# One drain per slot as the signal for TensorE's products, in a two-layer image network with gathered sampling

## The chip, the cores and the metric

The kernel runs on one core of a Trainium2 chip, as one program. The metric is the device time of one execution in microseconds; with one core, that core's time is the kernel's time. Lower is better.

## The reference

The input is four images `x` of 128 channels and 128 x 128 pixels, in float32, and the output has the same shape. Two layers follow each other; each has a convolution and a feed-forward part (FFN), both with a normalisation in front and a residual add behind. Cut to what matters:

```python
# layer 0
x = x + deform_conv(_ln_c(x), w_off, w_conv)      # 3x3 taps, sampled at learned places
t = t + moe(_ln_t(t), router_w, router_b, expert_w, expert_b)   # top 2 of 8 experts, per token
# layer 1
x = x + fft_conv(_ln_c(x), alphas, betas)         # mixes channels in the frequency domain
t = t + soft_moe(_ln_t(t), gate_w, gate_b, weight1, weight2)    # 64 experts take their top 8 tokens each

# deform_conv: offsets by a 3x3 convolution, then for each tap k
py, px = base_y + dy[k], base_x + dx[k]
sampled[k] = sum(weight(corner) * x[:, corner] for the four pixels around (py, px))
out = einsum('bckhw,ock->bohw', sampled, w_conv)
```

In layer 0 every pixel reads nine places of the image, each blended from four neighbouring pixels. The places depend on the data, so these reads are gathers. In layer 1's FFN each of 64 experts takes, over an image's 16,384 tokens, the eight with the highest gate.

## The kernel before

**Tiling.** The unit of work is a *slot*. A slot samples one row of 128 pixels at three of the nine taps. Each image has 32 groups of four rows, and each group has 12 slots (four rows by three sets of taps), so four images make 4 x 32 x 12 = 1536 slots. A class `Chunk` holds what a slot does:

- `gather` (L737): three indirect DMAs issued by GpSimd (POOL), one per tap, each fetching 128 places x 4 corners x 128 channels from a table in DRAM into the tile `g`. The pool of `g` has `AHEAD` = 7 buffers (L82, L245), so up to seven slots' gathers are in flight.
- `weighted` (L750) on VectorE (DVE) and `weighted_too` (L758) on ScalarE (ACT): each corner times its blending weight, in place in `g`. The tile `spread` holds the weights.
- `summed` (L766): twelve 128 x 128 transposes on TensorE, which add up the four corners of each tap in PSUM, in the tile `trg`. They are the last readers of `g`: after them the buffer is free for the gather of seven slots later.
- `moved` (L780): ACT copies `trg` to `sT` in SBUF. Every fourth `moved` starts `convolved`, in which TensorE multiplies `sT` by the weights of the convolution (`sums`).

What follows the sampling of a group (normalisations, routing, the eight experts `pe`, layer 1's mixing and gates `pq`), and the preparation of the next image's offsets and table, are Python generators called *jobs*. They are resumed slot by slot and put their matmuls, copies and vector work between those of the sampling, so that the whole kernel is one interleaved stream. Behind the last slot come the 64 experts of layer 1 for the last image, and a pass that turns the tokens back into channels and writes the output.

**What sets the order.** Nothing is reordered: `InOrder` (L91 to L103) wraps each engine and records every instruction with `keep_in_program_order` (L101, hence the "L101" in every row of the profile). Each engine's queue holds its instructions in the order in which Python issues them. The order inside a slot n is written out in the main loop (L1588 to L1636): `weighted` of slot n+1, `moved` of slot n-2, the jobs' due steps (`turns.steps`, L1603), `weighted_too` of n+1, `summed` of n, the jobs' matmuls (`turns.fills`, L1611), and last the gathers of slot n+7, by `next(source)` (L1635).

**PSUM and the two-slot hop.** A job's or a slot's products go to one of `BANKS` = 6 PSUM buffers (L83, L246); `fills` (L147) keeps the count of those in use. A job that has issued matmuls waits `turns.hop` slots before it issues what reads them. The hop is 2 in the slots (L1584) and 1 behind them (L1638). So by the written order, readers of a product come two slots after it.

**Synchronisation.** An instruction that another engine (or, for hazards, its own) depends on raises its engine's semaphore when it is done, and the dependent one waits for a value of it. The tile framework derives all these waits and updates from the tiles read and written. Before, 6022 of TensorE's 31,271 matmuls carry such an update.

Of the kernel before, what the change touches and what calls it, by code (L numbers as in the profile page):

```python
# [90 lines left out]
class InOrder:  # L91


    def __init__(self, tc, engine):
        self.tc, self.engine = tc, engine

    def __getattr__(self, name):
        issue = getattr(self.engine, name)

        def issued(*args, **kwargs):  # L100
            return self.tc.keep_in_program_order(issue(*args, **kwargs))  # L101

        return issued  # L103


class Engines:
    def __init__(self, tc):
        nc = tc.nc
        self.tensor, self.vector = InOrder(tc, nc.tensor), InOrder(tc, nc.vector)
        self.scalar, self.gpsimd = InOrder(tc, nc.scalar), InOrder(tc, nc.gpsimd)  # L110
        self.sync = InOrder(tc, nc.sync)

# [57 lines left out]
def runs_of(runs, first, step):  # L170


    if len({n for _, _, n in runs}) > 1:
        return [(slice(s, s + n), first(y, n)) for s, y, n in runs]
    (_, y, n), (_, z, _) = runs
    ap = first(y, n)
    dims = list(ap.ap)
    return [
        (
            slice(0, 2 * n),  # L180
            bass.AP(ap.tensor, ap.offset, [dims[0], [(z - y) * step, 2]] + dims[1:]),
        )
    ]
# [3 lines left out]
def metaformer_kernel(  # L187
# [16 lines left out]
    nc = tc.nc  # L204
# [33 lines left out]
    with ExitStack() as main:  # L238
# [15 lines left out]
        eng = Engines(tc)  # L254
# [5 lines left out]
        class Image:  # L260


            def __init__(self, b):
                self.b = b
                self.table = tabs.tile([TW * TC, 2 * P], F32, name=f"table{b}", tag="table")
                self.grid = self.table.rearrange("(i j) e -> i j e", j=TC)
                self.index = pw.tile([P, P, TAPS], I32, name=f"index{b}", tag="index")
                self.weight = {}
                self.xc = {}
                self.z = {}  # L270
                self.tails = {}


                self.read = self.normed = self.continued = self.sent = 0
                self.offsets = self.placed = self.known = 0
                self.left = 0
                self.direct = P // RB
                self.rooms = {}
# [381 lines left out]
        def table_of(im, pitch):  # L660

            base = turns.slot
            im.left = P // RB + 1 + P // CB
            for t in range(P // RB + 1):
                while turns.slot < base + int(t * pitch):
                    yield 1
                turns.start(block(im, t))

        def later_offsets(im):
            for t in range(im.direct, P // RB):  # L670
                turns.start(again(im, t))
                yield SPACE


        class Group:
# [6 lines left out]
            def begin(self):  # L682
                self.xg = pb.tile([P, 4, P], F32, name="xg", tag="xg")
                for s, rows in runs_of(
                    self.runs,
                    lambda y, n: x[self.b, :, y : y + n, :].rearrange("c y x -> c (y x)"),
                    P,
                ):
                    eng.sync.dma_start(
                        out=self.xg[:, s, :].rearrange("p s x -> p (s x)"), in_=rows  # L690
                    )
# [854 lines left out]
        def biases():  # L1546

            for whole, bias, to, n in (
                (HID, weight1[:, P, :], b1T, NJ),
                (P, weight2[:, HID, :], b2T.unsqueeze(1), 1),  # L1550
            ):
                rows = late.tile([E1, whole], F32, name="rows", tag="two", bufs=3)
                eng.sync.dma_start(out=rows, in_=bias)
                yield 3
                yield FILL
                pbt = bank([P, n, E1], "pbt")
                for j in range(n):
                    eng.tensor.transpose(
                        pbt[:, j, :],
                        rows.rearrange("e (p j) -> e j p", j=n)[:, j, :],  # L1560
                        ident[:E1, :E1],
                    )
                yield turns.hop
                eng.vector.tensor_copy(to, pbt)
# [22 lines left out]
        n = -1  # L1587
        while n < total + 3 or turns.jobs:  # L1588
            turns.slot = start + n
            b, k = divmod(n, slots)  # L1590
            if n == 0:
                turns.start(later_offsets(first))
            lag = 0 if b else SPACE * (P // RB - AFTER + 2)
            if k == lag and b + 1 < NB:
                images[b + 1] = Image(b + 1)
                images[b + 1].border()
                pitch = (slots - AHEAD - BLOCK - lag) / (P // RB)
                turns.start(table_of(images[b + 1], pitch))
            if n + 1 < total:
                chunk[n + 1].weighted()  # L1600
            if 0 <= n - 2 < total:
                chunk[n - 2].moved()
            turns.steps()  # L1603
            if n >= 0 and n + 3 < total and (n + 3) % 12 == 0:
                chunk[n + 3].row.group.weights((n + 3) // 12 % 2)
            if n + 1 < total and chunk[n + 1].shared:
                chunk[n + 1].weighted_too()
            if 0 <= n < total:
                chunk[n].summed()
                turns.fill()  # L1610
            turns.fills(0)  # L1611
            if n == LATE * slots:

                phase_a.close()
                late = main.enter_context(tc.tile_pool(name="late", bufs=2, side="right"))
                b1T = late.tile([P, NJ, E1], F32, name="b1T", tag="b1T", bufs=1)
                b2T = late.tile([P, E1], F32, name="b2T", tag="b2T", bufs=1)
                turns.start(biases(), later=True)
                part = lambda: late.tile([P, 2, HID], F32, name="w", tag="w", bufs=4)

                rooms = [[part(), part()], [part(), part()], flat_pads]
                rooms.append([pw.tile([P, 2, HID], F32, name="w", tag="index")])
                for _ in range(2):
                    rooms[-1].append(
                        pw.tile([P, 1, HID], F32, name="w", tag="weight", bufs=3 * P // CB // 2)
                    )
                middle = Experts(range(LATE), Weights(lambda i: rooms[i % 4]), 4, 2)
                middle.part = part
                middle.streams = 2
                middle.weights.load(4)  # L1630
                middle.start()
            if 0 <= n - 2 < total:
                chunk[n - 2] = None
            if 0 <= n and len(chunk) < total:
                chunk.append(next(source))  # L1635
            n += 1  # L1636
            if n == total + 2:
                turns.hop = 1  # L1638

                sampling.close()  # L1640
                own = main.enter_context(tc.tile_pool(name="own", bufs=OWN))

                flat = lambda w: w[:, 0:8, :].rearrange("p (n q) c -> p n (q c)", q=4)
                others = [
                    flat_pads,
                    [(late, f"{tile}{b}") for tile in ("tok", "share") for b in (1, 2)],
                    [flat(wconv_sb), flat(ew_sb)],
                ]

                def room(i):  # L1650
                    i %= OWN + 3 + len(LEFT)
                    if i < OWN:
                        return own.tile([P, EC, HID], F32, name="w", tag="w")
                    i -= OWN
                    if i == 1:
                        return [
                            pool.tile([P, 1, HID], F32, name="w", tag=tag, bufs=1)
                            for pool, tag in others[1]
                        ]
                    if i < 3:  # L1660
                        return others[i]
                    return [
                        pb.tile([P, n, HID], F32, name="w", tag=tag, bufs=bufs)
                        for tag, n, bufs in LEFT[i - 3]
                    ]

                ending = Ending(range(LATE, NB), Weights(room), OWN + 2, 1)
                ending.part = lambda: own.tile([P, 2, HID], F32, name="w", tag="w")
                ending.streams = OWN // 2
                ending.among = False  # L1670
                turns.start(ahead())
                ending.start()
# [39 lines left out]
```

## Time and profile before

| | before |
|---|---|
| median of three runs | 7361.9 us (7357.83 to 7363.09) |
| the profiled execution | 7358.05 us |
| its span, first to last instruction | 7356.1 us |
| TensorE's granted clock, mean | 0.896 |
| TensorE matmuls | 6006.3 us busy (82%), 31,271 instructions |
| VectorE | 4789.5 us (65%), 16,100 |
| GpSimd | 4432.3 us (60%), 4691 |
| ScalarE | 3707.7 us (50%), 9999 |
| bytes moved by DMA | 1524.69 MB, mean 207 GB/s |

All times are of one execution, taken by the hardware profiler. PE is TensorE's matmuls and PEld its weight loads. In a row of a group, "out<-in xcount | busy, mean ns | idle before, releaser" gives the tiles, the number of instructions, their busy time, the mean length of one, and how long the engine stood idle just before them, with what ended most of that. "issue" as releaser means that the profile shows nothing that the engine waited for; "remote" is a releaser without a name. Matmuls are pipelined: their ends are modelled, and their records overlap, so PE's busy share isn't its share of peak. Releasers are inferred from semaphore events.

### The profile page before, as it was taken

Reading aid. Unit: us, or ns where it says so; the run is one execution under the profiler, and the core shown is the slowest. Engines: PE = TensorE matmul, PEld = TensorE weight load, DVE = VectorE, ACT = ScalarE, POOL = GpSimd, SP = SyncE. Lnnn points to the kernel's source line nnn. Section 1 sums busy time; section 2 is a strip of 40 time slices with the busy share of each in tenths; the row PEclk is TensorE's granted clock in tenths of the full one; section 3 lists DMA queues with packets and bytes.
Section 4 is the critical chain, followed back from the end, with each engine's and each line's share of the span. In section 5 each row is a group of like instructions: output and inputs, shape, how many; then the busy total and the mean of one; then the engine's idle time right before and its main releaser. Section 6 shows DMA issues by size and latency. Waiting matters only on the chain. (4 is left out here: it accounts for less than half of the span.)

```text
span 7356.1 us, 103037 instructions
## 1 busy us (share of the span) xinstructions
PE 6006.3 (82%) x31271; PEld 3981.9 (54%) x31271; DVE 4789.5 (65%) x16100; ACT 3707.7 (50%) x9999; POOL 4432.3 (60%) x4691
## 2 busy tenths in 40 slices
PE   5788888887888888887888888888877788788885
PEld 3455555555555555555555555555555555555553
DVE  5466666676667666666667666667667665566663
ACT  4345555554555555554455555555444444444452
POOL 1666666666666666666666666666666665666641
PEclk7888999998898998998899999898898999899897
DMA  6666666666666666666666666666666677677777
GB/s 204 191 200 212 204 207 210 202 194 188 197 201 203 205 206 200 204 193 186 193 209 200 207 202 201 198 199 210 186 189 181 201 250 238 180 247 237 246 236 273
DMA packets 578917, 1524.69 MB, mean 207 GB/s; under 512 B 86424, under 2 KB 225408, under 8 KB 578368
## 3 DMA queue, kind: packets, MB, share of 16 engines
q0 software_dynamic: 369664, 1210.35, 55.0%
q1 hardware_dynamic: 206400, 299.36, 12.1%
q10 hardware_dynamic: 2304, 8.39, 0.3%
q8 instruction: 254, 4.16, 0.2%
q14 instruction: 295, 2.42, 0.1%
HBM read 1380.92 MB, written 136.85 MB: 206 GB/s over the span
## 5 line engine op out<-in xcount | busy, mean ns | idle before, releaser
L101 POOL DMA_INDIRECT g<-table,index x4608 | 4377.4, 950 | 2710.4 <-issue 1190.9
L101 PEld LDWEIGHTS trg<-ident,g 128*128 128x128 f32 x18432 | 2300.2, 150 | 1501.3 <-issue 1288.2
L101 PE MATMUL trg<-ident,g 128*128 128x128 f32 x18432 | 2575.2, 288 | 562.9 <-issue 465.9
L101 DVE SCALAR_TENSOR_TENSOR x<-pe,scaled,x 128x128 f32<-128x128 f32 x4048 | 1379.7, 341 | 1432.5 <-remote 644.6
L101 DVE TENSOR_TENSOR g<-g,spread 128x1024 f32<-128x1024 f32 (+1 forms) x1536 | 2129.1, 1387 | 202.4 <-DMA g<-table,index 90.0
L101 ACT COPY sT<-trg 128x384 f32<-128x384 f32 x1536 | 720.5, 472 | 2742.1 <-remote 1187.4
L101 PE MATMUL sums<-sT,wconv_sb 128*128 128x512 f32 x2304 | 1326.6, 658 | 53.1 <-issue 50.9
L101 ACT ACTIVATE g<-g,weight 128x128 f32<-128x128 f32 x4096 | 1306.3, 394 | 1.9 <-DMA g<-table,index 1.7
L101 PE MATMUL pe<-ew_sb,x1T 128*128 128x512 f32 x2048 | 1163.6, 649 | 147.0 <-issue 88.6
L101 PEld LDWEIGHTS sums<-sT,wconv_sb 128*128 128x128 f32 x2304 | 435.1, 208 | 518.9 <-issue 516.5
L101 PEld LDWEIGHTS pe<-ew_sb,x1T 128*128 128x128 f32 x2048 | 343.7, 205 | 261.1 <-issue 182.3
L101 ACT ACT_TABLE_LOAD x270 | 346.4, 1283 | 23.5 <-DVE nmax L101 9.8
L101 PE MATMUL sums<-xg,ident 128*128 128x512 f32 x256 | 163.8, 726 | 125.8 <-ACT x1T L101 96.8
L101 DVE TENSOR_TENSOR x<-ps,x 128x512 f32<-128x512 f32 x128 | 88.1, 688 | 264.5 <-remote 119.6
L101 PE MATMUL po<-pad,woff_sb 128*64 128x512 f32 x768 | 216.1, 645 | 17.8 <-issue 11.0
L101 DVE TENSOR_TENSOR x<-x,pe 128x512 f32<-128x512 f32 x128 | 87.0, 679 | 217.8 <-remote 130.4
L101 PE MATMUL pl<-rw_sb,x1T 128*128 128x8 f32 x1024 | 143.9, 256 | 98.2 <-issue 88.7
L101 ACT ACTIVATE tn<-x,d_nb,d_rs 128x128 f32<-128x128 f32 x512 | 211.2, 487 | 5.5 <-DVE x L101 2.6
L101 ACT ACTIVATE xn<-x,c_nb,c_rs 128x128 f32<-128x128 f32 x512 | 210.6, 485 | 4.7 <-issue 1.8
L101 PEld LDWEIGHTS pl<-rw_sb,x1T 128*128 128x128 f32 x1024 | 147.3, 213 | 98.5 <-issue 88.6
L101 ACT ACTIVATE ent<-raw,a_nb,a_rs 128x128 f32<-128x128 f32 x448 | 185.0, 485 | 7.6 <-remote 3.8
L101 PE MATMUL pe<-eb_sb,gT 32*128 32x512 f32 x256 | 169.4, 740 | 20.0 <-issue 14.6
(227 smaller groups left out, 5130.9 us busy)
## 6 DMA issues: line engine op xcount, KB each, us to landing
g<-table,index POOLq DMA_INDIRECT x4608
table<-ent SPq DMA_DIRECT2D x64, 1024.0 KB
xc<-in_x SPq DMA_DIRECT2D x64, 512.0 KB
w<-x_d SPq DMA_DIRECT2D x64, 512.0 KB
xg<-in_x SPq DMA_DIRECT2D x124, 256.0 KB
x_d<-x SPq DMA_DIRECT2D x124, 256.0 KB
out<-w SPq DMA_DIRECT2D x48, 512.0 KB
w<-in_weight SPq DMA_DIRECT2D x40, 512.0 KB
```

The source lines that it names most:

```text
L101: return self.tc.keep_in_program_order(issue(*args, **kwargs))
```

## The change

TensorE's wrapper becomes `Fenced`, a subclass of `InOrder`. At the start of each slot `begin` opens a group named after the slot's number. Every TensorE instruction issued in the slot is added to it, as one whose finishing isn't signalled by itself (`add_to_no_dep_group`). At the slot's end `end` issues a `drain` on TensorE, an instruction that lets what stands before it finish, keeps it in program order, and declares it the fence of the group (`declare_fence`): whoever depends on a matmul of the group waits for the drain's semaphore update in its place. The drain stands behind `turns.fills(0)`, and so behind all of the slot's matmuls, and ahead of the gathers of slot n+7. A slot without matmuls gets none. Matmuls ahead of the main loop have no group and keep their own updates. The computation, the tiles, the pools and the order of all other instructions stay.

```diff
+class Fenced(InOrder):
+    def __init__(self, tc, engine):
+        super().__init__(tc, engine)
+        self.group, self.number, self.some = None, 0, False
+
+    def __getattr__(self, name):
+        issue = super().__getattr__(name)
+
+        def issued(*args, **kwargs):
+            made = issue(*args, **kwargs)
+            if self.group is not None:
+                self.tc.add_to_no_dep_group(self.group, made.ins)
+                self.some = True
+            return made
+
+        return issued
+
+    def begin(self):
+        self.number += 1
+        self.group, self.some = f"products{self.number}", False
+
+    def end(self):
+        if self.some:
+            fence = self.tc.keep_in_program_order(self.engine.drain())
+            self.tc.declare_fence(fence.ins, group=self.group)
+        self.group = None
+
 class Engines:
...
-        self.tensor, self.vector = InOrder(tc, nc.tensor), InOrder(tc, nc.vector)
+        self.tensor, self.vector = Fenced(tc, nc.tensor), InOrder(tc, nc.vector)
...
             turns.slot = start + n
+            eng.tensor.begin()
...
             turns.fills(0)
+            eng.tensor.end()
             if n == LATE * slots:
```

## The prediction

> **What bounds the kernel now.** I read the page first: engine totals, the strip of 40 slices, the costliest groups. The strip (GpSimd's row is shown) is flat from the second slice to the last but one, so one steady stage holds the time: the 1,536 sampling slots.
>
> ```profile
> PE 6006.3 (82%) x31271; PEld 3981.9 (54%) x31271; DVE 4789.5 (65%) x16100; ACT 3707.7 (50%) x9999; POOL 4432.3 (60%) x4691
> ...
> POOL 1666666666666666666666666666666665666641
> ...
> L101 POOL DMA_INDIRECT g<-table,index x4608 | 4377.4, 950 | 2710.4 <-issue 1190.9
> ...
> L101 PE MATMUL trg<-ident,g 128*128 128x128 f32 x18432 | 2575.2, 288 | 562.9 <-issue 465.9
> ...
> L101 ACT COPY sT<-trg 128x384 f32<-128x384 f32 x1536 | 720.5, 472 | 2742.1 <-remote 1187.4
> ```
>
> No engine is full. POOL's gathers take 4377 us, but POOL idled 2710 us just before them. ACT's copy of a slot's sums out of PSUM (sT) has more idle time in front of it than any other group of ACT, put down to "remote", a releaser that the profile couldn't name. POOL's tile view puts the gathers from 135.3 to 7123.6 us: 6988 us, or 4.55 us for each of 1,536 slots. Inside a run of gathers one starts every 1.25 us (0.95 + 0.30 idle), so 4608 x 1.25 = 5760 us would do. The other 1228 us are pauses in which POOL waits for TensorE to free a buffer. So I read one cycle in the timeline (start, length, engine, operation; in brackets the idle time before and its releaser):
>
> ```profile
> 2993.63 1.53 PE L101 MATMUL trg<-ident,g 128*128 128x128 f32 x12 [0.46 <-issue]
> ...
> 2995.86 1.02 PE L101 MATMUL pe<-ew_sb,x1T 128*128 128x512 f32 x2
> ...
> 2999.60 0.95 POOL L101 DMA_INDIRECT g<-table,index  x1 [0.30 <-issue]
> ...
> 3000.12 1.02 PE L101 MATMUL pe<-ew_sb,x1T 128*128 128x512 f32 x2
> 3002.14 0.48 ACT L101 COPY sT<-trg 128x384 f32<-128x384 f32 x1 [2.21 <-PE pe L101]
> 3002.17 0.35 DVE L101 SCALAR_TENSOR_TENSOR x<-pe,scaled,x 128x128 f32<-128x128 f32 x1 [3.00 <-PE pe L101]
> ...
> 3002.79 0.94 POOL L101 DMA_INDIRECT g<-table,index  x1 [2.24 <-ACT sT L101]
> ```
>
> A slot's products are read two slots later, so the copy at 3002.14 reads the trg that ended at 2995.16, DVE's the pe that ended at 2996.88, ACT's lq at 3002.51 the pq of 2996.02. ACT, DVE and POOL stand still, and so does TensorE from 3001.14 (its next weight load starts at 3005.25), though all these products had been done for 5 to 7 us. All start within 0.7 us: the semaphore updates of six products came in one burst at 3002.06. The last gather before had ended at 3000.55.
>
> I then paired every reader that had only a TensorE product to wait for, and started out of idleness, with its product's last matmul. ACT's 898 started 4.6 us (median) after that matmul's modelled end, DVE's 339 3.7 us after it, the quickest 37 ns. Readers of ACT's and DVE's results start 32 to 53 ns after them when nothing else holds them. The lateness has a place: through the first 140 us and after 7150 us, where no gathers run, products are read 37 ns after their end.
>
> ```profile
> 7348.24 1.87 PE L101 MATMUL pf<-ident,w 128*128 128x128 f32 x8 [0.55 <-DMA w<-x_d]
> 7349.36 0.59 ACT L101 COPY w<-pf 128x512 f32<-128x512 f32 x1 [1.90 <-PE pf L101]
> ...
> 7350.15 0.69 DVE L101 COPY w<-pf 128x512 f32<-128x512 f32 x1 [1.67 <-PE pf L101]
> ```
>
> Here the fourth matmul ended at 7349.32 and ACT starts at 7349.36. In the steady stage the gathers come in 599 trains of 3, 6 or 9. TensorE's updates run at 0.02 to 0.3 per us in the first microsecond after a train's last gather, and at 5 to 7 per us from 1.4 us on. So while POOL issues gathers TensorE's update path is nearly shut; it opens 1.4 us after POOL has stopped; and POOL stops only because it waits for such an update. That loop is the bound.
>
> **The change, part by part.** In the built programs the matmuls stand in the same order; only synchronisation changes. Matmuls with an update fall from 6,022 to 153. 1,601 drains on TensorE come in. Waits set apart as instructions of their own grow by 438 on TensorE, 381 on POOL and 23 on ACT, and fall by 70 on DVE and 66 on SP.
>
> Removed updates. The Trainium skill (TensorE: Matmul & The Clock Gate, "The cost: per-tile semaphore tail") lets increments serialise at 26.3 ns each; 6022 - 1754 = 4268 fewer would be 112 us. The trace has no such cost on TensorE: the transposes follow each other every 0.109 us with or without an update. I take 0.
>
> The drain itself. Queued behind it on TensorE is the whole next slot, its weight loads too, which now run up to 0.1 us ahead. The nearest row is the one drain at the program's end: it ended at 7350.154, 0.05 us after the last matmul's modelled end (7350.107). A 128-column matmul's record is 0.27 us long where the next would start at 0.109, so waiting for its end costs 0.16 us. Then 0.05 for the drain, 0.06 from a satisfied wait to the first matmul (7348.18 to 7348.24), and 0.055 because the first matmul after a stop is followed 0.164 and not 0.109 us later. Sum 0.32 us, over 1601 slots 512 us. Here the same page speaks against the change ("Single matmul latency"): a matmul alone takes (398 + N)/2.4 ns, one in a stream N/2.4 + 2.5, so each emptying costs 163 ns or, as my estimate, 261 us. I take the trace's 512, as it holds the restart. No reason makes it a gain; from above, 438 waits at 51 ns (TensorE's own row for such a wait) add 22 us.
>
> What hides it. TensorE's work at full clock is 25,100 narrow matmuls x 0.109 + 6,150 of 512 columns x 0.43 = 5380 us, some 5220 of it in the gather stretch, so 3.40 us per slot, and 3.72 with the drain, against 4.55 now. So the bubble lies in time that TensorE now waits away. If the waiting goes, TensorE (3.72) and POOL (3.75) bind together, and the bubble has no cover left.
>
> The moved signal. Readers now wait for the slot's end, not their product. They come two slots later by the schedule (in the last 230 us, one), so this costs nothing while they are less than a slot behind. TensorE waits for its own drains too, for 1,220 of them the one before the last: a whole slot old, so free if drains signal promptly.
>
> What is decisive is how late a drain's update is in the middle of a train, which no row shows. From below: 0.05 us, as at the end. From above: as late as a matmul's own, 1.4 us after the train. The same skill's Perfetto Trace Analysis has the update of a matmul leave when PSUM acknowledges it, and a drain's leave from the sequencer ("Tensor Engine Instruction", "Sequencer-only Instruction"). By the first rule there'd be nothing to win: the readers lose up to a slot and TensorE 261 to 512 us. The rows of 4.6 us contradict it here. I take the prompt end. TensorE goes on issuing matmuls while earlier updates are pending, so the work isn't held, only its report. ACT's and DVE's reports pass in the same microseconds, so semaphores as such aren't held. And TensorE's waits end 52 ns after ACT's updates, so its sequencer isn't held.
>
> **Sum.** Each slot then costs the larger of 3.72 and 3.75 us plus what two equal, uneven partners lose to each other. TensorE's slots vary from 2 to 6 us, and its clock, 0.896 now, will not reach 1. I allow 8%: 4.05 us. 1536 x 4.05 = 6221; head 135 and tail 232 as before, 10 for drains in the tail: 6598 span, and 2 us around it (7358.05 against 7356.1): 6600. The profiled run lies 0.05% under the median 7361.9, so no correction.
>
> **Rivals.**
> 1. The drain is held as well (slower). The mechanism: its update, or its seeing the array empty, waits till 1.4 us after the train. One freed buffer lets POOL issue 3 gathers, 3.76 us, and TensorE's 3.4 us slot ends inside them, so every slot takes 3.76 + 1.4 = 5.16 us: 1536 x 5.16 + 377 = 8300. If only the update is late and TensorE seldom waits for it, the present cycle stays and the bubble counts in part: 7400 to 7700. It decides as soon as a drain's signal takes over 0.8 us (4.55 - 3.76) in a train. For it: everything TensorE now reports is late. Against it: the three observations above.
> 2. The gain is eaten. Drains are prompt, but each costs more than its row, since emptying stops the issue running ahead. At 0.9 us per drain TensorE needs 4.3, at the present clock 4.5 us per slot: 7100 to 7350. For it: 82% busy already. Against: the end's drain, at 0.05 us.
> 3. Nothing happens: the lateness isn't on the path. Against it are POOL's 1228 us of pauses.
>
> **Numbers.** Prompt drains: 0.66, 6200 to 7000 (5760 + 377 is the floor by POOL). Gain eaten: 0.05. No change within 0.2%, about what a measurement here can tell: 0.03. Held drains: 0.26, of it a good third below 8000. To leave out at most 2 in 10 the range goes to 8000. Faster 0.71, same 0.03, slower 0.26.
>
> **What would show it.** Right: the idle time before gathers falls from 2710 to under 1700 us, their stretch from 6988 to about 6220; ACT's sT loses its 1187 us on "remote"; TensorE's drains last well under 1 us beyond their matmuls; its clock rises over 0.93. Wrong: drains that end 1.4 us after POOL's last gather, TensorE idle behind them, gathers in trains of three.

## The result, and the profile after

The changed kernel took 8030.1 us (median of four runs, 8019.4 to 8032.0) against 7362.5 us for the kernel before (7357.8 to 7371.6): 1.0902 times, 95% interval 1.0883 to 1.0921. The forecast was 6600 us, with a range of 6200 to 8000. The profiled execution took 8032.03 us, its span 8030.3.

The page of the changed kernel, with the rows that answer to those shown of before:

```profile
PE 6178.6 (77%) x31271; PEld 4010.7 (50%) x31271; DVE 4823.8 (60%) x16100; ACT 3736.9 (47%) x9999; POOL 4434.0 (55%) x4691
...
POOL 2555555555555555555555555555555555555541
...
L101 POOL DMA_INDIRECT g<-table,index x4608 | 4379.1, 950 | 3369.8 <-issue 1138.4
...
L101 ACT COPY sT<-trg 128x384 f32<-128x384 f32 x1536 | 733.4, 478 | 4054.2 <-PEq L132 3741.2
...
L101 PE MATMUL sums<-sT,wconv_sb 128*128 128x512 f32 x2304 | 1486.6, 731 | 1078.3 <-issue 1026.9
```

Every engine's share fell. The idle time before the gathers rose from 2710 to 3370 us, before the copies to `sT` from 2742 to 4054. The releaser of the copies has a name now: PEq L132, the drain. And TensorE itself stands still. The matmuls `sums`, which often open a slot's work after a drain, have 1078 us of idle time before them. In the kernel before it was 53 us:

```profile
L101 PE MATMUL sums<-sT,wconv_sb 128*128 128x512 f32 x2304 | 1326.6, 658 | 53.1 <-issue 50.9
```

A drain is an instruction of TensorE's sequencer. The view of line 132, where all drains are issued, gives its length (min/median/max) and who waited for it (us, times):

```profile
L132 PEldq DRAIN  x1601: 357/3823/16580, 143.0 to 8023.0; - x178
...
  ACT sT L101: 3741.2, 1196
  DVE x L101: 2404.6, 890
```

A drain's record can begin while matmuls of its slot still run. The one in the timeline below begins at 3650.89, and the slot's transposes run from 3650.57 to 3652.07. So its length is not its cost; what matters is how long it lasts beyond the last matmul. The timeline shows one case (start, length, engine, operation):

```profile
3650.57 1.50 PE L101 MATMUL trg<-ident,g 128*128 128x128 f32 x12 [0.25 <-ACT spread L101]
...
3650.80 0.95 POOL L101 DMA_INDIRECT g<-table,index  x1 [0.30 <-issue]
...
3652.05 0.95 POOL L101 DMA_INDIRECT g<-table,index  x1 [0.31 <-ACT g L101]
...
3658.38 0.95 POOL L101 DMA_INDIRECT g<-table,index  x1 [0.30 <-issue]
3660.43 0.48 ACT L101 COPY sT<-trg 128x384 f32<-128x384 f32 x1 [6.88 <-PEq L132]
...
3660.46 2.07 PE L101 MATMUL sums<-sT,wconv_sb 128*128 128x512 f32 x2 [8.39 <-issue]
```

The slot's last transpose ended at 3652.07. GpSimd was issuing a train of nine gathers (gathers with only short gaps between them), the last of which ended at 3659.33. The drain's record runs to 3660.40. It ended 8.3 us after the last transpose and 1.1 us after that gather. Then ACT and TensorE both start within 0.06 us. Without the drain nothing in TensorE's own queue would have kept it from the next slot during those 8 us.

I made this sum for each drain of the gather stretch. Of 1521 drains, 896 ended within 0.3 us of their last matmul (27 ns in the mean). The other 625, called late here, ended 0.3 to 11.4 us after it (2.3 in the median), and 402 of them between 1.2 and 1.8 us behind the last gather of a train. TensorE's time in that stretch then splits as follows (us; "work" is each matmul's record less the 0.163 us by which records overlap, the rest is time between matmuls):

| | before, 200 to 7100 | after, 200 to 7750 |
|---|---|---|
| work, at the clock as granted | 5440 | 5597 |
| waiting elsewhere | 1460 | 53 |
| drains: last matmul's way through the array | | 247 |
| drains: beyond that matmul's end | | 1472 |
| drains: from their end to the next matmul | | 177 |

TensorE's waits for other engines are nearly gone, as forecast. In their place it waits for its own drains: 1896 us, of which 1472 are held drains and 424 are emptying and restart. Work and drains together fill the stretch, so TensorE has become the bound.

### The profile page after: what moved, and what is told of

It is laid out like the page before. It is cut to its first block, busy times and chain, and to the rows that moved or that the text cites. A ratio compares the mean times of both kernels' runs of the same rounds, so it can differ in the third digit from the quotient of the medians.

```text
span 8030.3 us, 105344 instructions
## 1 busy us (share of the span) xinstructions
PE 6178.6 (77%) x31271; PEld 4010.7 (50%) x31271; DVE 4823.8 (60%) x16100; ACT 3736.9 (47%) x9999; POOL 4434.0 (55%) x4691
## 5 line engine op out<-in xcount | busy, mean ns | idle before, releaser
L101 PEld LDWEIGHTS trg<-ident,g 128*128 128x128 f32 x18432 | 2399.6, 156 | 1422.7 <-issue 1121.7
L101 PE MATMUL trg<-ident,g 128*128 128x128 f32 x18432 | 2608.0, 298 | 453.2 <-DMA g<-table,index 213.5
L101 PE MATMUL sums<-sT,wconv_sb 128*128 128x512 f32 x2304 | 1486.6, 731 | 1078.3 <-issue 1026.9
L101 PEld LDWEIGHTS sums<-sT,wconv_sb 128*128 128x128 f32 x2304 | 395.1, 209 | 1770.0 <-issue 1758.8
L101 PE MATMUL pe<-ew_sb,x1T 128*128 128x512 f32 x2048 | 1098.3, 619 | 2.1 <-PEq L132 0.9
L101 PE MATMUL po<-pad,woff_sb 128*64 128x512 f32 x768 | 191.1, 604 | 3.9 <-ACT pad L101 2.6
L101 PEld LDWEIGHTS sums<-xg,ident 128*128 128x128 f32 x256 | 42.1, 207 | 259.4 <-issue 225.4
L101 DVE BATCH_NORM_STATS2 a_st<-raw 128x6 f32<-128x128 f32 x512 | 136.3, 278 | 36.7 <-ACT raw L101 36.3
L101 PE MATMUL pe<-eb_sb,gT 32*128 32x512 f32 x256 | 152.8, 677 | 0.2 <-PEq L132 0.2
```

## The experiments

Theory A: a drain ends only when the reports of the matmuls before it are in; these are held while GpSimd issues gathers, and TensorE stands behind the drain. Its rivals: B, that the cost is that readers wait for the slot's end in place of their product; C, that it is the emptying of the array; D, that DMA traffic, and not GpSimd, holds the reports.

One thing came in between. The runs went to several chips. The kernel before took 6165 to 6174 us on two of them (e1 to e6), and 7265 to 7361 us on two others (e7 to e14), as in the first measurement. Each ratio below is to the kernel before on the same chip; a single run gets none. I call the second kind *holding* chips, because late drains show on them only. Only one of the four was measured on more than one occasion, so whether this belongs to the chip or to the occasion wasn't separated.

| run | this, us | before, us | ratio (interval) | late drains | TensorE idle beyond drains' matmuls, us |
|---|---|---|---|---|---|
| e1_bare_drain | 6183.1 | 6174.3 | 1.0014 (1.0005 to 1.0024) | 0 of 1506 | 73 |
| e2_before_sp | 5379.1 | 6174.3 | 0.8713 (0.8699 to 0.8728) | | |
| e3_after_sp | 5897.5 | 6174.3 | 0.9551 (0.9535 to 0.9567) | 0 of 1494 | 33 |
| e4_after_one | 5893.6 | 6174.3 | 0.9544 (0.9528 to 0.9560) | 0 of 1494 | 33 |
| e5_after_again | 6181.1 | 6164.6 | 1.0026 (1.0015 to 1.0037) | 0 of 1518 | 33 |
| e6_bare_drain_again | 6173.8 | 6164.6 | 1.0016 (1.0006 to 1.0025) | 0 of 1506 | 73 |
| e7_before_again | 7265.2 | 7272.2 | one run | | |
| e8_two_drains | 8563.1 | 7272.2 | one run | 706 of 3016 | 1526 |
| e9_bare_drain_early | 7772.0 | 7272.2 | one run | 622 of 1513 | 1358 |
| e10_bare_drain_3 | 7850.0 | 7361.4 | 1.0665 (1.0634 to 1.0696) | 693 of 1514 | 1446 |
| e11_after_sp_again | 5901.5 | 7361.4 | 0.8018 (0.7994 to 0.8041) | 2 of 1493 | 37 |
| e12_after_one_again | 5904.5 | 7361.4 | 0.8022 (0.7998 to 0.8045) | 5 of 1492 | 42 |
| e13_train_of_three | 8943.1 | 7349.5 | one run | 37 of 1502 | 64 |
| e14_two_gathers | 6206.6 | 7349.5 | one run | 191 of 1486 | 250 |

The last two columns are worked out from each run's trace, in its gather stretch; late is over 0.3 us. Empty cells: the kernel has no drains in its slots.

**Is it the waiting readers, or TensorE's stop? A bare drain at the slot's end (e1, e6, e10).** Products keep their own updates, nobody waits for the drain:

```diff
-            if self.group is not None:
-                self.tc.add_to_no_dep_group(self.group, made.ins)
-                self.some = True
+            self.some = self.group is not None
...
-            fence = self.tc.keep_in_program_order(self.engine.drain())
-            self.tc.declare_fence(fence.ins, group=self.group)
+            self.tc.keep_in_program_order(self.engine.drain())
```

> A drain ends each slot as in the changed kernel, but every product keeps its own update and readers wait for that, as before. Theory A (a drain only ends once the reports of the matmuls before it have come, those are held while GpSimd issues gathers, and TensorE stands still behind it): the cost doesn't depend on who waits for the drain, so 7900 to 8200 us. Rival B (the cost is that readers wait for the slot's end in place of their own product): that is gone, only emptying and restart are left, 247 + 177 us in the trace of after: 7400 to 7800 us.

> The kernel with a bare drain per slot, and products with their own updates, again. On a chip that holds the reports, theory A: 7900 to 8200 us, rival B: 7400 to 7800 us. On a chip that doesn't: 6183 us as before.

> The bare drain at the slot's end again, products with their own updates, in the hope of a chip that holds TensorE's reports (the kernel before at 7270 to 7360 us). There, theory A: the same stops of TensorE as in the changed kernel, whoever waits for the drain: 1.07 to 1.11 times before, 7800 to 8150 us. Rival B: without readers at the drain nothing but emptying is left, 1.00 to 1.04 times before; with the early drain it was 7772 against 7272, so a time clearly under that (under 7600) would say that the place at the slot's end is cheap and its use as the signal is what costs. On a chip that doesn't hold them: 6183 us.

The first two ran on chips that don't hold and could tell nothing between A and B: 1.0014 and 1.0016. The third ran on a holding chip and took 7850 us or 1.0665 times before: inside A's span in us, just under it as a ratio (1.07), and well outside B's (1.00 to 1.04). Its page has the copies to `sT` waiting for their product again, and TensorE waiting as in the changed kernel:

```profile
L101 ACT COPY sT<-trg 128x384 f32<-128x384 f32 x1536 | 731.7, 476 | 3357.5 <-PE trg L101 1419.5
L101 PE MATMUL sums<-sT,wconv_sb 128*128 128x512 f32 x2304 | 1427.8, 705 | 1060.9 <-issue 1002.4
```

The 1061 us of idle time before `sums` are close to those of the changed kernel (1078), and 1446 us beyond the drains stand against its 1472. So the hold doesn't depend on who waits for the drain; B falls as the main cause. This run also shows what a drain waits for, as its products keep their own updates: 594 of its 693 late drains end 32 to 40 ns after a recorded update of TensorE, and where nothing is held (e1) it is 33 ns in the median too. (Not every update is recorded: 4998 of 6067.) Late drains and late reports come together, as A says.

The drain as a signal adds the rest, from 1.0665 to 1.0902, as far as two measurements with nearly the same time of before (7361.4 and 7362.5) can be set side by side. In the two splits, work differs by 143 us (5454 here, 5597 there; the granted clock is 0.912 here and 0.897 there), the time from a drain's end to the next matmul by 28 and that beyond the matmuls by 26. Why the clock is lower with fewer updates stays open.

**Another place (e9).** The kernel before, with a bare drain ahead of the jobs' matmuls:

```diff
                 chunk[n].summed()
+                tc.keep_in_program_order(nc.tensor.drain())
                 turns.fill()
```

> The kernel before with a bare drain right behind the twelve transposes of each slot, ahead of the jobs' matmuls; products keep their own updates. On a chip that doesn't hold the reports: 6165 to 6190 us, as with the bare drain at the slot's end. On a chip that holds them, theory A (TensorE stands behind a held drain): 7700 to 8200 us; rival B (only waiting for the slot's end costs): 7360 to 7700 us.

On a holding chip it took 7772 us against 7272 (one run of each), inside A's span and outside B's: the place at the slot's end isn't what costs.

**Gathers away from GpSimd (e2, e3, e11).** In the kernel before and in the changed one, plain DMAs by SyncE replace all gathers. They move as many bytes, from places that don't depend on the data, so these kernels leave the deformable sampling out. The edit, cut:

```diff
-                    eng.gpsimd.indirect_dma_start(
...
+                    t = self.row.group.im.table
+                    eng.sync.dma_start(
+                        out=self.g[:, i].rearrange("p s c -> p (s c)"),
+                        in_=bass.AP(t.tensor, t.offset + self.row.y * TC * 2 * P,
+                                    [[2 * P, P], [1, 4 * P]]),
+                    )
```

> The kernel before, with all three gathers of a slot replaced by plain DMAs of the same size that SyncE issues, from the same table, at places that don't depend on the data: the deformable sampling is left out. Theory A: without gathers on GpSimd TensorE's updates come at once, and TensorE's work (5440 us in the gather stretch) sets the time: 6000 to 6400 us. Rival D (it is the DMA traffic that holds TensorE's updates, not GpSimd's issuing): the traffic stays, so 7100 to 7500 us.

> The changed kernel with the same plain DMAs by SyncE (deformable sampling left out). Theory A: all drains are prompt, so only emptying and restart are paid, some 424 us over the kernel before with the same DMAs: 6400 to 6800 us. Rival C (the emptying itself is the main cost): at least 600 us over it. Rival D: about 8000 us, as the traffic still holds the drains.

> The changed kernel with all gathers replaced by plain DMAs of SyncE, again (deformable sampling left out). On a chip that holds TensorE's reports: theory A, that it takes GpSimd's issuing of gathers to hold them: all drains within 0.1 us of their last matmul, 5900 to 6300 us. Rival D, that the DMA traffic or its reports do it, whoever issues it: drains late by 1 us in the mean, 7400 us or more. On a chip that doesn't hold them: 5897 us.

The levels of e2 and e3 came out 500 to 620 us under the spans that I had written. I had built on 5440 us of work, with the first chip's slower clock in it (granted clock 0.896, here 0.985); the work in e2's gather stretch is 4865 us. Their difference is what they were made for: 5897.5 - 5379.1 = 518 us for 1601 drains, 0.32 us each, with no hold and nothing to hide them. That is under C's 600, and refutes C for the result: of TensorE's 1896 us only 424 are this price. On a holding chip (e11) the changed kernel with these DMAs took 5901.5 us, the same as on the other (5897.5), with 2 late drains of 1493. So without gathers by GpSimd there is no hold, and the chips differ in nothing else of that size.

**One gather per slot, then two (e4, e12, e14).** In the changed kernel, with the same plain DMA for the other taps; the sampling is left out for these.

> The changed kernel with one gather per slot by GpSimd and two plain DMAs by SyncE (deformable sampling left out for two of three taps). In the changed kernel no drain was held that came within 3 us of the start of a train of gathers, nearly all that came later than 4.5 us were. Theory A: trains of one gather (0.95 us) stay below that, drains are prompt, 6400 to 6800 us as with no gathers. If any gather shuts the path until 1.4 us after it: some drains are held by up to 2 us, 6900 to 7400 us. Rival D: about 8000 us.

> The changed kernel with one gather per slot on GpSimd and two plain DMAs on SyncE, again (deformable sampling left out for two of three taps). On a chip that holds the reports: theory A with the 3 us of grace after the start of a train: prompt drains, 5900 to 6300 us. If a single gather closes the path until 1.4 us after it: 6400 to 7200 us. Rival D: 7400 us or more. On a chip that doesn't hold them: 5894 us.

> The changed kernel with two gathers per slot on GpSimd and one plain DMA on SyncE (deformable sampling left out for one of three taps): trains of 2.2 us where one slot is released at a time, 4.7 us where two are. Theory A with 3 us of grace, on a chip that holds the reports: few drains are late (under 200 us in all) and TensorE sets the time, 5900 to 6150 us. If a shorter train holds too: 6300 us or more. On a chip that holds none: 5900 us.

The bytes that a slot moves are the same in all of these. The page and the view of line 132 of e12, on a holding chip:

```profile
L101 POOL DMA_INDIRECT g<-table,index x1536 | 1457.2, 949 | 4162.5 <-DVE x L101 910.1
```

```profile
L132 PEldq DRAIN  x1601: 358/2772/5232, 140.9 to 5893.1; - x178
...
  ACT sT L101: 1891.2, 1046
```

The longest drain fell from 16.6 to 5.2 us, late drains from 625 to 5, and the time is that of a chip that doesn't hold (5904.5 and 5893.6; the latter some 500 us under e4's span, for the reason given above). D falls. Nor do late drains wait until all the gathers' data have landed: in the changed kernel's trace 13 packets of the gathers' DMA queue are under way, in the median, when a late drain ends, and none for 28 of the 625.

With two gathers per slot 191 drains were late and the time rose to 6207 us, between the two spans that I had set (up to 6150, and 6300 or more). So the "3 us of grace" is no fixed limit, and e4's expectation had misread the changed kernel's trace. There, counting a train as ended by a pause of over 0.6 us, 68 of 491 drains whose last matmul ended within 3 us of a train's start were late, and 413 of 428 that came over 4.5 us after the start and still in the train.

**All gathers, but no long train (e13).** In the changed kernel, other GpSimd work behind each slot's gathers:

```diff
+                for _ in range(3):
+                    eng.gpsimd.iota(
+                        by_i, pattern=[[1, CB], [1, 3], [0, 3]], base=0, channel_multiplier=0
+                    )
```

> The changed kernel, all gathers on GpSimd, with three index-making operations (iota, 551 ns each in the trace of before) behind each slot's three gathers, so that no train is longer than 3.5 us and about 1.9 us lie between trains, in which GpSimd is busy with other work. GpSimd then needs 3.75 + 1.7 = 5.4 us per slot, which alone gives 1536 x 5.4 + 370 = 8700 us. Theory A, that issuing gathers without a break for over 3 us holds the reports: on a chip that holds them, TensorE's idle time beyond the end of a drain's matmuls falls from 1472 to under 150 us, and the time is 8600 to 8900 us. Rival E, that any work of GpSimd holds them: drains stay late, the slot takes at least 1 us more, over 9500 us. On a chip that holds none, 8700 us and no late drain.

GpSimd's timeline, on a holding chip:

```profile
4002.68 0.99 POOL L101 DMA_INDIRECT g<-table,index  x1 [0.23 <-issue]
4003.97 0.95 POOL L101 DMA_INDIRECT g<-table,index  x1 [0.31 <-issue]
4005.23 0.95 POOL L101 DMA_INDIRECT g<-table,index  x1 [0.30 <-issue]
4006.19 1.79 POOL L101 IOTA by_i<- 128x144 int32 x3
4008.21 0.99 POOL L101 DMA_INDIRECT g<-table,index  x1 [0.23 <-issue]
```

A slot takes 5.53 us of GpSimd here (4008.21 - 4002.68), and 5.58 in the mean, where I had reckoned 5.4, so 8943 us in place of 8900 at most. It is far too long to be of use, but all 4608 gathers are there, GpSimd hardly pauses, and drains end with their matmuls: 64 us beyond them in all, against 1472. So it is gathers in close succession that hold the reports, not any work on GpSimd (rival E) and not the number of gathers. Their mean rate alone isn't it either: e13 and e14 both issue 0.54 or 0.53 gathers per us, with 37 and 191 late drains. The pauses between e14's trains, mostly of two gathers, are shorter (1.6 us in the median, in e13 2.0). How the length of a train and that of the pause share in it was not separated.

**Before and after on both kinds of chips (e5, e7), and two drains (e8).** e8 adds the early drain of e9 to the changed kernel.

> The changed kernel again, beside the kernel before on the same chip. In the last four runs the kernel before took 6174 us, not 7362: on that chip the reports of TensorE were not held (its idle time beyond the end of a drain's matmuls was 73 us in the run with bare drains, against 1472 us in the first trace of after). If this run is on such a chip, theory A: emptying and restart cost some 420 us of TensorE, of which GpSimd's 1.25 us per gather (5760 us) hides most: 6200 to 6450 us against 6174 of before. If the chip holds the reports again: 8030 against 7362 us. Rival B (readers wait for the slot's end, and that costs by itself): at least 6600 us on a chip that does not hold them.

> The kernel before, unchanged, for a trace of it on this chip. Theory A, with the chips' difference added: where the chip doesn't hold TensorE's reports the readers start within 50 ns of their product and GpSimd issues its gathers in long trains, 6165 to 6175 us in all; where it holds them the trace looks like the first one, with trains of 3 to 12 gathers, 7360 us.

> The changed kernel with a second drain per slot, right behind the twelve transposes. On a chip that doesn't hold the reports, TensorE's own need in the gather stretch rises from 5017 + 474 us to about 5017 + 948 = 5965, over GpSimd's 5760: if a drain's price is 0.3 us and GpSimd's gathers had been its cover, the time rises from 6181 to 6350 to 6450 us. If the second drain is free because the array is soon empty anyway: 6181. On a chip that holds them: over 8300 us.

The changed kernel on a chip that doesn't hold took 6181 us against 6165, 19 us under A's span and far under B's 6600 or more. Its views of the gathers, of line 132, and of the timeline around one drain:

```profile
L101 POOL DMA_INDIRECT g<-table,index x4608: 940/946/1486, 134.2 to 5945.2; - x192
```

```profile
L132 PEldq DRAIN  x1601: 313/2757/5422, 142.7 to 6172.9; - x178
```

```profile
3001.66 1.02 PE L101 MATMUL pe<-ew_sb,x1T 128*128 128x512 f32 x2
...
3001.89 0.94 POOL L101 DMA_INDIRECT g<-table,index  x1 [0.30 <-issue]
...
3002.76 1.12 PE L101 MATMUL sums<-sT,wconv_sb 128*128 128x512 f32 x2
```

In the middle of a train the slot's last matmul ends at 3002.68 and the next slot's first starts at 3002.76: the drain ended at once. The gathers run from 134.2 to 5945.2 us, 1.26 us each, nearly without a pause (the longest train, again with no pause over 0.6 us, has 3507). GpSimd is the bound there, and the drains' 474 us of TensorE lie in its shadow. Where the remaining 16 us are I can't say, as there is no trace of the kernel before from such a chip. e7, the kernel before on a holding chip, shows the same picture as the first trace: 607 trains against 624, and between 200 and 7000 us 868 us in TensorE pauses of over 1 us against 974. e8 fell on a holding chip as well, so it doesn't say when the drains' price leaves GpSimd's shadow; there the second drain per slot brought 8563 us (over 8300 had been expected), against before's 7272, with some 770 us of emptying and restart and 1526 us of hold.

## Why the prediction was wrong

It was wrong in one step, the one it called decisive: "I take the prompt end." I had seen that TensorE's reports were held while GpSimd issued gathers, and had three reasons why a drain's shouldn't be. The first was the error: "TensorE goes on issuing matmuls while earlier updates are pending, so the work isn't held, only its report." That is true of the matmuls of the kernel before. But a drain ends only with these reports (e10: 594 of 693 late ones within 32 to 40 ns of one). So it turned a late report, which TensorE's next matmuls didn't wait for, into a stop of TensorE; e10 shows that this happens with nobody waiting for the drain. In the sum, the term of 0.05 us from the last matmul's end to the drain's measured 0.97 us in the mean (1472 / 1521). The other two reasons, that ACT's and DVE's reports pass and that TensorE's sequencer isn't held, were true and didn't bear on it. Of the two rules weighed there, that a matmul's update leaves when PSUM acknowledges it and a drain's from the sequencer (the Trainium skill, Perfetto Trace Analysis, "Tensor Engine Instruction" and "Sequencer-only Instruction"), the second was no reason for a prompt end: the signal does leave at the drain's end (its recorded update comes 13 ns later in the median), but the end itself was up to 11.4 us late.

The nearest row, the one drain at the program's end (0.05 us), was measured where no gathers run. I had noted for the matmuls' updates that they are prompt just there, and should have read the drain's row with the same caution.

By its other steps:

- **The bound of before** was right. Where reports aren't held the kernel before takes 6165 to 6174 us: the loop of held reports costs it some 1190 us, and GpSimd's gathers are next, as 5760 us plus head and tail (135 + 232) had said.
- **The drain's price** where it is prompt was right: 0.32 us forecast, 0.28 measured in the changed kernel ((247 + 177) / 1521), 0.32 by e3 against e2. The 163 ns set beside it is an estimate, and the formula that it takes for a stream is another section's (the Trainium skill, TensorE: Matmul & The Clock Gate, "Back-to-back issue gap"), which gives it for isolated matmuls; the sum didn't use it. The 112 us for removed updates was an estimate as well, from a passage on packed tiles, and no run here separates that gain.
- **What hides it** was wrong in the other direction: "the bubble has no cover left" once the waiting goes, and the 8% for "what two equal, uneven partners lose to each other", don't fit e5. With prompt drains GpSimd's gathers still covered the drains, and the time was 6181, not 6600 us: TensorE's need there, 5017 us of work and 474 of drains in the gather stretch, stayed under GpSimd's 5760.
- **Rival 1** is what happened, at 0.26 in my chances. Its mechanism holds, its size was too large: it had every slot's drain held, and 8300 us in all. The gathers ran from 134.6 to 7781.7 us, 4.98 us per slot, since only 625 of 1521 drains were held. So the time fell 30 us outside a range whose upper end cut this rival in two.
- **Signs named in advance**: "drains that end 1.4 us after POOL's last gather, TensorE idle behind them, gathers in trains of three" are there: 495 of 1014 trains have three gathers, against 52 of 624 before.

## What to carry to other kernels

In these runs a drain was no cheaper signal than the updates it replaced: it waited for the same reports, and the whole queue behind it waited too. If a product's report is late for a reason outside its engine, ask what stands still because of it today, and don't let the producer join. Take the price of an instruction from a row in the stage where it will stand; a row from the tail says nothing of a stage in which something else is late. This kernel, whose bound was a late report, differed by a fifth between chips (7362 and 6165 us), so compare on one chip only.

## What the runs showed of the hardware

The kernel before takes 6165 to 6174 us on two chips and 7265 to 7362 us on the others. No trace of it comes from the first two, but those of e1 and e3 to e6 do, and they have no late drain. On the others TensorE's reports are held while gathers follow each other closely: 625 of 1521 drains late in the changed kernel, none of 1518 in e5.

On the holding chips the records of semaphore events are thin as well: of some 9280 increments of each of the eight semaphores that gathers raise, 2421 to 2808 are recorded in the first trace of before, 3931 to 4399 in that of after, and 9273 to 9281 in that of e5. So events of several sources seem to crowd each other on these chips; that this is the cause of the hold was not shown, and no run here tells what makes a chip one kind or the other. One rival stands untested: every time here comes from an execution under the profiler, which records these very events, so no run tells whether the reports are held without it.

TensorE's granted clock goes with the hold, 0.892 to 0.900 for the kernel before on holding chips and 0.957 to 0.964 on the others. It isn't the chip's own: without GpSimd's gathers it is 0.987 on a holding chip (e11).
